# Wide loads, rows read eight tiles ahead, and results fetched a step sooner in a cross-attention and mixture-of-experts kernel

## The chip, the cores and the metric

The kernel runs on one core of a Trainium2 chip. The metric is the device time of one execution in microseconds. Three runs of the kernel before gave 608.56 us as median (607.83 to 609.25).

The core has a tensor engine (PE, which does the matrix products), a vector engine (DVE), a scalar engine (ACT), a general engine (POOL, GpSimd) and a sync engine (SP) that here only issues transfers. Transfers between device memory and on-chip memory run on 16 DMA engines. SP and ACT issue to hardware queues, which the profile numbers q1 and q10; POOL's transfers appear as q0.

## The reference

All tensors are float32. There are 4 batches of 512 tokens with 512 features, and a context of 1024 rows per batch.

```python
def layer(x, ctx):                      # x (4, 512, 512), ctx (4, 1024, 512)
    n = layernorm(x)
    q = fmap(n @ Wq.T)                  # fmap(a) = a + 1 if a > 0 else exp(a); 16 heads of 32
    gate = sigmoid(n @ Wg.T + bg)
    k, v = split(ctx @ Wkv.T)
    k = fmap(k)
    kv = einsum('bhsd,bhse->bhde', k, v)
    z = 1 / (einsum('bhld,bhd->bhl', q, k.sum(s)) + 1e-6)
    x = x + (einsum('bhld,bhde->bhle', q, kv) * z * gate) @ Wo.T
    n = layernorm(x)
    w, sel = top_k(n @ Wr, 2)           # 8 experts
    w = softmax(w)
    return x + sum(w[i] * (n @ We[sel[i]] + be[sel[i]]) for i in (0, 1))
```

## The kernel before

Work is tiled by 128 rows. The program first does the attention of the four batches in order. For each batch, `kv_tiles` (L374) goes over eight context tiles: it loads a tile two steps ahead (`load_ctx`, three buffers), makes keys and values from it with 8 matmuls each for keys and for values (`half_tile`, L310), and adds their product to a running sum. Then come queries and gates from the transposed, normalized x (`query`, `gate`), the attention products (`products`), the output projection (`attention_out`, L477), and the routing (`choose`, L526, and `dispatch`, L580). `dispatch` writes each token's normalized row twice into the array `stream` in device memory, once in the region of each of its two experts, by indirect writes that POOL issues.

The experts then work on tiles of 128 rows of `stream` (`run`, L738). The first 17 tiles (EARLY) belong to the first three batches and run inside and after the last batch's attention. The 18 late tiles that are always there (SURE) follow once the last batch has been dispatched and the list of their rows has been computed on DVE (`listed`, L680). For each tile, SP reads the row number from that list, then issues four loads of 64 KB and one of 1 KB (`rows`, L742). DVE transposes the tile in 32x32 blocks (`turned`, L776), PE does four chunks of matmuls with the expert's weights (`expert`, L796), DVE adds the bias, and POOL scatters the 128 result rows to the array `result` (L818).

The results are collected while the late tiles run: at steps of a hand-written plan (`begins`, L932) the two results of 128 tokens are fetched (`fetch`, L871), added with their gates (`add`, L896) and stored (`store`, L911). A list `READ` (L46) says how many tiles must be done before a fetch. The last two fetches wait for all results.

All of SP's transfers stay in the program's order. `tc.keep_in_program_order` and `tc.issue_after` fix further orders by hand; the rest of each engine's order is found when the program is built. The buffers of expert rows are the context tiles' three and two of the values'.

Three layouts matter here. `load_rows` (L132) fills a weight in four loads of 32 partitions each, with 4 x 512 numbers in each partition; the expert weights use the same layout in a loop of their own (L382). The tiles of the experts are loaded in the same manner, four loads of 32 partitions with 4 x 128 numbers each (L756). `spread_moments` (L277) writes the means and the reciprocal deviations of x to device memory in two transfers of single numbers and reads them back in four, so that every partition has those of its rows.

Of the kernel before, what the change touches and what calls it, by code (L numbers as in the profile page):

```python
# [9 lines left out]
F32 = mybir.dt.float32  # L10
I32 = mybir.dt.int32
U32 = mybir.dt.uint32
AF = mybir.ActivationFunctionType
ALU = mybir.AluOpType
# [3 lines left out]
P = 128  # L18
B, L, S, D = 4, 512, 1024, 512
E, F = 8, 512  # L20
HD = 32
NC = D // P
NT = L // P
# [30 lines left out]
def xattn_moe_kernel(  # L54
# [32 lines left out]
    result = dram.tile([NOWHERE + 2 * L, F], F32, name="result")  # L87


    moments = dram.tile([B, HD, NT, P // HD, 2], F32, name="moments")  # L90


    def matmul(**operands):
# [8 lines left out]
    def load(dst, src):  # L102
        latest["load"] = nc.sync.dma_start(out=dst, in_=src)  # L103
        tc.keep_in_program_order(latest["load"])
# [27 lines left out]
    def load_rows(dst, w):  # L132


        for i in range(NC):
            load(dst[ts(i, HD)], w.rearrange("(c f) i n -> i f c n", f=HD)[i])

    wkv_sb = wpool.tile([P, NC, 2 * D], F32, tag="wkv", name="wkv_sb")
    wq_sb = wpool.tile([P, NC, D], F32, tag="wq", name="wq_sb")
# [3 lines left out]
    nc.gpsimd.memset(wr_sb, 0.0)  # L143
    bg_sb = wpool.tile([P, NC], F32, name="bg_sb")
    we_sb = wpool.tile([P, E, NC, F], F32, name="we_sb")
    we_rows = we.rearrange("e (c f) i n -> e i f c n", f=HD)

    ctx_tiles = {}

# [104 lines left out]
    def layernorm_stats(tiles):  # L254
        mv = small.tile([P, NT, 2], F32, tag="mv", name="mv")
        for t in range(NT):
            st = small.tile([P, 6], F32, tag="st", name="st")
            nc.vector.bn_stats(st, tiles[t])
            nc.vector.bn_aggr(mv[:, t, :], st)
        rstd = small.tile([P, NT], F32, tag="rstd", name="rstd")  # L260
        nc.scalar.activation(rstd, mv[:, :, 1], AF.Sqrt, bias=eps_sb)
        nc.vector.reciprocal(rstd, rstd)
        return mv, rstd

    def normalize(dst, xt, t, mv, rstd):
        nc.vector.tensor_scalar(
            dst, xt, mv[:, t, 0:1], rstd[:, t : t + 1], ALU.subtract, ALU.mult
        )

    def transposed(dst, src):  # L270

# [4 lines left out]

    def spread_moments(b, tiles):  # L277

        mv, rstd = layernorm_stats(tiles)
        for k, of in enumerate((mv[:, :, 0], rstd)):  # L280
            nc.gpsimd.dma_start(
                out=moments[b, :, :, :, k].rearrange("t n j -> j t n"), in_=of
            )
        ln = small.tile([P, NT, P // HD, 2], F32, tag="ln", name="ln", bufs=1)
        for i in range(NC):
            nc.gpsimd.dma_start(
                out=ln[ts(i, HD)].rearrange("t n j k -> t (n j k)"),
                in_=moments[b].rearrange("t n j k -> t (n j k)"),
            )
        return ln  # L290

    def normalized_T(xT, t, blocks, ln):

        rows = blocks[:, ts(t, D)].rearrange("p (j f) -> p j f", f=P)
        with tc.issue_after(latest["map"].ins):
            for j in range(P // HD):
                nc.vector.tensor_scalar(
                    rows[:, j], rows[:, j], ln[:, t, j, 0:1], ln[:, t, j, 1:2],
                    ALU.subtract, ALU.mult,
                )  # L300
            nc.vector.transpose(
                xT[:, :, ts(t, P)].rearrange("p c (j t) -> p j c t", t=HD),
                rows.rearrange("p j (c f) -> p j c f", f=HD),
            )
# [69 lines left out]
    def kv_tiles(b, lo, hi, between=None, inside=None):  # L374
        for s in range(lo, hi):
            nxt = (b, s + 2) if s + 2 < NS else (b + 1, s + 2 - NS)
            if nxt[0] < B and nxt not in loaded_ctx:
                loaded_ctx.add(nxt)
                ctx_tiles[nxt] = load_ctx(*nxt)
            if b in (1, 2) and s % 2 == 0:  # L380
                e = (b - 1) * E // 2 + s // 2
                for i in range(NC):  # L382
                    load(we_sb[ts(i, HD), e], we_rows[e, i])
            for e in (s,) if b else (2 * (s - NS // 2), 2 * (s - NS // 2) + 1):
                if e >= 0:
                    set_empty(b, e)
            if s == 0:
                sums[b] = pkv.tile([P, NC, 2 * P], F32, tag="kvs", name="kvs")
            k = made.pop(s) if s in made else keys(b, s)
            if (b, s) == (0, 0):  # L390
                made[1] = keys(0, 1)
            if inside is not None and s == lo:
                inside()
            v = values(b, s)
            if s > 0:
                kv_add(sums[b], s - 1, *pending[b])
            pending[b] = k, v
            if between is not None:
                between(s - lo)
        if hi == NS:  # L400
            kv_add(sums[b], NS - 1, *pending[b])
# [121 lines left out]

    routed = {}

    def choose(b, mv, rstd):  # L526

        rows = []
        batch = work.tile([P, NT, ROW], F32, tag="row", name="rows", bufs=1)
        for t in range(NT):  # L530
            row = batch[:, t, :]
            normalize(row[:, 0:D], xs[b][t], t, mv, rstd)
            nc.gpsimd.tensor_copy(row[:, D : D + 1], home[:, b * NT + t : b * NT + t + 1])
            rows.append(row)

# [202 lines left out]
    def run(lists, lo, n, early):  # L738
        why = "clamped to the tiles of the streams and to the experts where it is computed"
        no_i, row_i, ranked = lists  # L740

        def rows(j):  # L742


            row = nc.values_load(
                row_i[0:1, j : j + 1], [ET.SP], min_val=0, max_val=SLOTS,
                skip_runtime_bounds_check_because=why,
            )
            if (j if early else j + EARLY) % 5 < 3:
                xg = cpool.tile([P, ROW], F32, tag="cT", name="xg")  # L750
            else:
                xg = kvpool.tile([P, ROW], F32, tag="v", name="xg", bufs=2)
            of = small.tile([P, 2], F32, tag="of", name="of", bufs=8)
            rows_of = stream[ds(row, P), :]
            parts = []
            for i in range(NC):  # L756
                parts.append(
                    (
                        xg[ts(i, HD), 0:D].rearrange("t (j f) -> t j f", j=NC),
                        rows_of[:, ts(i, P)].rearrange("(j t) f -> t j f", t=HD),  # L760
                    )
                )
            parts.append((of, rows_of[:, D:ROW]))
            for dst, src in parts:
                load = nc.sync.dma_start(out=dst, in_=src)  # L765
                latest["load"] = load
                if early:
                    behind(load, written["stream"][: 2 * NT * (B - 1)], "tokens of the tile")
                    early_loads.append(load)
                    for put in scatters.get(B - 1, []):  # L770
                        tc.declare_no_dep(load.ins, put.ins, reason=full_already)
                else:
                    behind(load, written["stream"], "tokens of the tile")
            return xg, of
# [55 lines left out]


        loaded, ready = [], []
        if early:
            turned_rows = big.tile([P, 4, NC, P], F32, tag="xT", name="turned_rows")

        def after(what):
            return tc.issue_after(latest[what].ins) if what in latest else nullcontext()

        for j in range(lo - 5, n):
            if j + 5 < n:  # L840
                with after("load"):
                    loaded.append(rows(j + 5))
            if j >= lo:
                with after("turn"):
                    expert(j, *ready.pop(0))
            if j + 3 >= lo and loaded:
                with after("y"):
                    ready.append(turned(j + 3, *loaded.pop(0)))
            yield
# [76 lines left out]
    def plan(step, *what):  # L926
        at_step.setdefault(min(step, SURE), []).append(what)

    def queue_of(step):
        return nc.gpsimd if step < SURE - 5 else nc.scalar  # L930

    begins = (-3, -2, -1, 0, 5, 6, 7, 8, 10, 11, 14, 15, SURE - 2, SURE - 2)  # L932
    for g, (lo, hi, most) in enumerate(READ):
        for t in range(lo, hi):
            plan(begins[t], fetch, t, most, queue_of(begins[t]), g)
    for t, begin in enumerate(begins):
        step = begin + (3 if begin < SURE - 4 else SURE)
        plan(step, add, t, gates if step < SURE else gates_end)
        plan(step + 1, store, t, queue_of(step + 1))

    def also(j):
        for what, *of in at_step.pop(j, []):
# [3 lines left out]
    xT = new_xT()  # L946
    kv_tiles(0, 0, 3)
    for g, a, b, n in turned:
        load(bg_sb[b : b + n, g : g + 1], bg[a : a + n, g : g + 1])
        load(wo_sb[b : b + n, g, :], wo[a : a + n, g, :])  # L950
    ln = spread_moments(0, xs[0])

# [2 lines left out]
            normalized_T(xT, t, blocks, ln)  # L955

    kv_tiles(0, 3, NS, between)
    kv_blocks(sums[0])
    for b in range(B):
        more = b + 1 < B  # L960
# [60 lines left out]
            for _ in range(3):  # L1021
                next(early)
        attention_out(b, aT)
        choice = choose(b, *layernorm_stats(xs[b]))
        if more:

            def between(i):
# [47 lines left out]
    nc.vector.tensor_copy(soon_i, worst)  # L1075

    late = run(late_list, 0, SURE, False)
    for j in range(-5, SURE):
        if j < 0:
            next(early)  # L1080
        next(late)
        with tc.issue_after(latest["y"].ins):
            also(j)
# [77 lines left out]
```

## Time and profile before

| | |
|---|---|
| median of the runs | 608.56 us |
| the profiled execution's own time | 610.59 us |
| its span in the profile | 608.9 us |
| mean granted clock of PE | 0.984 |
| PE busy | 576.7 us, 95% |
| DVE, ACT, POOL busy | 289.6, 109.3, 120.5 us |
| moved by DMA | 109.87 MB, mean 180 GB/s |
| SP's queue q1, share of 16 engines | 49.0% |
| first matmul starts, last one ends | 4.45 us, 589.2 us |
| four narrow loads of each expert weight, eight experts | 32 loads of 256 KB |
| loads of expert rows | 140 of 64 KB |

How it is read: the page gives each engine's busy time, then the span in forty slices of 15.2 us with the busy tenths of each. The DMA row is the mean busy share of the 16 engines. A view of the chain follows the work that ended last back to what released it. A timeline gives the instructions of one engine with the idle time before them in brackets and what ended it. The DMA view of a window gives for each queue the packets, the MB, and the time that its packets took as a share of 16 engines.

### The profile page before, as it was taken

Reading aid. Unit: us, or ns where it says so; the run is one execution under the profiler, and the core shown is the slowest. Engines: PE = TensorE matmul, PEld = TensorE weight load, DVE = VectorE, ACT = ScalarE, POOL = GpSimd, SP = SyncE. Lnnn points to the kernel's source line nnn. Section 1 sums busy time; section 2 is a strip of 40 time slices with the busy share of each in tenths; the row PEclk is TensorE's granted clock in tenths of the full one; section 3 lists DMA queues with packets and bytes.
Section 4 is the critical chain, followed back from the end, with each engine's and each line's share of the span. In section 5 each row is a group of like instructions: output and inputs, shape, how many; then the busy total and the mean of one; then the engine's idle time right before and its main releaser. Section 6 shows DMA issues by size and latency. Waiting matters only on the chain.

```text
span 608.9 us, 6440 instructions
## 1 busy us (share of the span) xinstructions
PE 576.7 (95%) x1780; PEld 270.0 (44%) x1780; DVE 289.6 (48%) x732; ACT 109.3 (18%) x168; POOL 120.5 (20%) x289
## 2 busy tenths in 40 slices
PE   7989999999999999999999999999999999998950
PEld 3545544454555435445543454554344443443420
DVE  2215254354317443541564355128765579473863
ACT  1311241220313321122242121221300110000000
POOL 4230021000001510000061100003211237444630
PEclk9989999999999999999999999999999999999995
DMA  8979995374490698627338660952255444889866
GB/s 283 166 122 355 340 197 48 116 238 131 121 277 19 140 240 261 190 87 209 103 140 147 236 203 5 315 221 108 89 119 121 121 122 167 251 235 295 243 225 212
DMA packets 78933, 109.87 MB, mean 180 GB/s; under 512 B 13229, under 2 KB 39853, under 8 KB 78768
## 3 DMA queue, kind: packets, MB, share of 16 engines
q1 hardware_dynamic: 68112, 79.91, 49.0%
q0 software_dynamic: 8336, 24.29, 12.2%
q10 hardware_dynamic: 2448, 5.24, 2.6%
q8 instruction: 15, 0.25, 0.2%
q14 instruction: 22, 0.18, 0.1%
HBM read 50.19 MB, written 59.96 MB: 181 GB/s over the span
## 4 chain that ended last, share of the span: by engine, by line
PE 74%; DMA 9%; DVE 6%; SPq 4%; issue 4%; POOL 1%; DVEq 0%; ACTq 0%; POOLq 0%
PE pk L94 18%; PE pv L94 16%; PE pq L94 9%; PE po L94 9%; PE pg L94 7%; PE pe L94 5%; PE kvs L94 4%; DMA xg<-stream 4%; DMA cT<-in_cT_dram 3%; SPq L765 2%; SPq L103 1%; PE pn L94 1%; PE pt L97 1%; DMA result<-y,to 1%; DMA of<-stream 1%
## 5 line engine op out<-in xcount | busy, mean ns | idle before, releaser
L94 PE MATMUL pk<-wkv_sb,cT 128*128 128x512 f32 x256 | 119.4, 611 | 6.4 <-DMA cT<-in_cT_dram 6.4
L94 PE MATMUL pv<-wkv_sb,cT 128*128 128x512 f32 x256 | 115.2, 593 | 0.0
L250 DVE TENSOR_SCALAR ex<-pk 128x512 f32<-128x512 f32 x32 | 22.1, 692 | 135.1 <-PE pk L94 135.1
L94 PEld LDWEIGHTS pv<-wkv_sb,cT 128*128 128x128 f32 x256 | 48.4, 190 | 62.3 <-issue 59.8
L94 PEld LDWEIGHTS pk<-wkv_sb,cT 128*128 128x128 f32 x256 | 48.0, 196 | 60.9 <-issue 53.4
L94 PE MATMUL pe<-we_sb,xgT 128*128 x144 | 62.8, 594 | 3.9 <-DVE xgT L782 3.9
L94 PE MATMUL pe<-we_sb,turned_rows 128*128 x136 | 60.4, 596 | 1.9 <-DVE turned_rows L782 1.5
L94 PE MATMUL pg<-xT,wg_sb 128*128 128x512 f32 x128 | 56.7, 595 | 0.0
L94 PE MATMUL pq<-xT,wq_sb 128*128 128x512 f32 x128 | 56.6, 596 | 0.0
L94 PE MATMUL po<-wo_sb,aT 128*128 128x512 f32 x128 | 55.6, 592 | 0.0
L818 POOL DMA_INDIRECT result<-y,to x35 | 36.4, 1041 | 94.0 <-DVE y L814 91.3
L251 ACT ACTIVATE ex<-ex 128x512 f32<-128x512 f32 x48 | 30.2, 629 | 137.5 <-DVE ex L250 117.3
L330 POOL MEMSET v<- 128x4 f32 x32 | 3.3, 108 | 245.4 <-PE kvs L94 245.3
L94 PEld LDWEIGHTS pe<-we_sb,xgT 128*128 128x128 f32 x144 | 27.1, 190 | 39.4 <-issue 32.2
L624 POOL DMA_INDIRECT stream<-rows,slot x32 | 32.9, 1027 | 51.7 <-DVE acc L587 22.2
L94 PEld LDWEIGHTS kvs<-v,k 128*128 128x128 f32 x256 | 33.3, 191 | 16.0 <-issue 14.2
L94 PEld LDWEIGHTS pe<-we_sb,turned_rows 128*128 128x128 f32 x136 | 25.2, 190 | 34.0 <-issue 29.9
L94 PEld LDWEIGHTS pg<-xT,wg_sb 128*128 128x128 f32 x128 | 24.0, 190 | 32.1 <-issue 32.1
L94 PEld LDWEIGHTS po<-wo_sb,aT 128*128 128x128 f32 x128 | 24.1, 190 | 29.2 <-issue 28.7
L94 PEld LDWEIGHTS pq<-xT,wq_sb 128*128 128x128 f32 x128 | 23.8, 190 | 27.3 <-issue 27.3
L94 PE MATMUL kvs<-v,k 128*128 128x129 f32 x256 | 34.1, 275 | 0.0
L252 DVE SCALAR_TENSOR_TENSOR k<-pk,ex 128x512 f32<-128x512 f32 x32 | 22.1, 691 | 21.6 <-ACT ex L251 21.6
(183 smaller groups left out, 459.7 us busy)
## 6 DMA issues: line engine op xcount, KB each, us to landing
stream<-empty SPq DMA_DIRECT2D x24, 1028.0 KB
stream<-empty SPq DMA_DIRECT2D x8, 1285.0 KB
xg<-stream SPq DMA_DIRECT2D x140, 64.0 KB
we_sb<-in_we_dram SPq DMA_DIRECT2D x32, 256.0 KB
cT<-in_cT_dram SPq DMA_DIRECT2D x31, 256.0 KB
y<-result POOLq DMA_DIRECT2D x10, 512.0 KB
x<-in_x_dram SPq DMA_DIRECT2D x16, 256.0 KB
blocks<-in_x_dram SPq DMA_DIRECT2D x16, 256.0 KB
```

Of the source, the lines that this page charges most:

```text
L94: tc.keep_in_program_order(nc.tensor.matmul(**operands))
L97: tc.keep_in_program_order(nc.tensor.transpose(dst, src, ident))
L103: latest["load"] = nc.sync.dma_start(out=dst, in_=src)
L250: nc.vector.tensor_scalar(ex, src, 0.0, None, ALU.min)
L251: nc.scalar.activation(ex, ex, AF.Exp)
L252: latest["map"] = nc.vector.scalar_tensor_tensor(dst, src, 0.0, ex, ALU.max, ALU.add)
L330: nc.gpsimd.memset(v[:, :, P : P + 1], 1.0)
L624: put = nc.gpsimd.indirect_dma_start(out=stream, out_offset=bass.IndirectOffsetOnAxis(ap=slots[i][:, t, :], axis=0), in_=rows[t], in_offse ...
L765: load = nc.sync.dma_start(out=dst, in_=src)
L818: put = nc.gpsimd.indirect_dma_start(out=result, out_offset=bass.IndirectOffsetOnAxis(ap=home_i, axis=0), in_=y, in_offset=None, bounds_ch ...
```

## The change

- `load_rows` loads chunk by chunk: four loads of 128 partitions with 512 numbers each, in place of four of 32 partitions. The expert weights go through it as well. A tile of expert rows is loaded in four loads of 32 of its rows each, spread over 128 partitions.
- The late tiles are loaded eight tiles ahead in place of five. Four further buffers come from the row buffer of the last batch's `choose` (`more`).
- The reciprocal deviations are put beside the means, and one transfer writes both to device memory, in runs of eight numbers.
- The loads of `bg` leave SP's queue for POOL's.
- The fetches of token tiles 4 to 9 move one step ahead, those of 10 and 11 two steps; the stores of tiles 8 and 9 go to SP's queue, and tiles 10 and 11 are added and stored within the steps.

```diff
@@ wide loads of weights
-        for i in range(NC):
-            load(dst[ts(i, HD)], w.rearrange("(c f) i n -> i f c n", f=HD)[i])
+        for c in range(NC):
+            load(dst[:, c, :], w[ts(c, HD)].rearrange("f i n -> i f n"))
...
-                for i in range(NC):
-                    load(we_sb[ts(i, HD), e], we_rows[e, i])
+                load_rows(we_sb[:, e], we[e])
@@ statistics
-    moments = dram.tile([B, HD, NT, P // HD, 2], F32, name="moments")
+    moments = dram.tile([B, HD, P // HD, NT, 2], F32, name="moments")
...
-        rstd = small.tile([P, NT], F32, tag="rstd", name="rstd")
-        nc.scalar.activation(rstd, mv[:, :, 1], AF.Sqrt, bias=eps_sb)
-        nc.vector.reciprocal(rstd, rstd)
-        return mv, rstd
+        dev = small.tile([P, NT], F32, tag="rstd", name="dev")
+        nc.scalar.activation(dev, mv[:, :, 1], AF.Sqrt, bias=eps_sb)
+        nc.vector.reciprocal(mv[:, :, 1], dev)
+        return mv
...
-        for k, of in enumerate((mv[:, :, 0], rstd)):
-            nc.gpsimd.dma_start(
-                out=moments[b, :, :, :, k].rearrange("t n j -> j t n"), in_=of
-            )
+        nc.gpsimd.dma_start(out=moments[b].rearrange("t j n k -> j t (n k)"), in_=mv)
@@ late tiles
+        many_ahead = not early and lo == 0
...
-            if (j if early else j + EARLY) % 5 < 3:
+            if many_ahead and (j - lo) % 9 < 4:
+                xg = more[:, (j - lo) % 9, :]
+            elif (j - lo) % 9 < 7 if many_ahead else (j if early else j + EARLY) % 5 < 3:
                 xg = cpool.tile([P, ROW], F32, tag="cT", name="xg")
...
-            for i in range(NC):
+            for j in range(P // HD):
                 parts.append(
                     (
-                        xg[ts(i, HD), 0:D].rearrange("t (j f) -> t j f", j=NC),
-                        rows_of[:, ts(i, P)].rearrange("(j t) f -> t j f", t=HD),
+                        xg[:, ts(j, P)],
+                        rows_of[ts(j, HD), 0:D].rearrange("t (i f) -> i t f", i=NC),
                     )
                 )
...
+        ahead = 8 if many_ahead else 5
+        if many_ahead:
+            more = work.tile([P, NT, ROW], F32, tag="row", name="more", bufs=1)
...
-        for j in range(lo - 5, n):
-            if j + 5 < n:
+        for j in range(lo - ahead, n):
+            if j + ahead < n:
                 with after("load"):
-                    loaded.append(rows(j + 5))
+                    loaded.append(rows(j + ahead))
...
     late = run(late_list, 0, SURE, False)
+    for _ in range(3):
+        next(late)
@@ results
-    def queue_of(step):
-        return nc.gpsimd if step < SURE - 5 else nc.scalar
+    def queue_of(step, behind=nc.scalar):
+        return nc.gpsimd if step < SURE - 6 else behind
 
-    begins = (-3, -2, -1, 0, 5, 6, 7, 8, 10, 11, 14, 15, SURE - 2, SURE - 2)
+    begins = (-3, -2, -1, 0, 4, 5, 6, 7, 9, 10, 12, 13, SURE - 2, SURE - 2)
...
-        plan(step + 1, store, t, queue_of(step + 1))
+        plan(step + 1, store, t, queue_of(step + 1, nc.sync if step < SURE - 4 else nc.scalar))
@@ bias of the gate
-        load(bg_sb[b : b + n, g : g + 1], bg[a : a + n, g : g + 1])
         load(wo_sb[b : b + n, g, :], wo[a : a + n, g, :])
...
     kv_tiles(0, 3, NS, between)
+    for g, a, b, n in turned:
+        nc.gpsimd.dma_start(out=bg_sb[b : b + n, g : g + 1], in_=bg[a : a + n, g : g + 1])
```

## The prediction

> **What bounds the kernel now.** I read the page first, for the engine shares and the forty slices.
>
> ```profile
> span 608.9 us, 6440 instructions
> ...
> PE 576.7 (95%) x1780; PEld 270.0 (44%) x1780; DVE 289.6 (48%) x732; ACT 109.3 (18%) x168; POOL 120.5 (20%) x289
> ...
> PE   7989999999999999999999999999999999998950
> ...
> DMA  8979995374490698627338660952255444889866
> ```
>
> TensorE is busy in all but 32 us. What an edit can save lies in the gaps: 4.45 us before the first matmul, a gap near 38 us, small ones after 515 us, and the 19.7 us after the last matmul. DMA is nearly full at the start (first six slices) and in the late tiles (slices 34 to 37). Between, it has room.
>
> Then the chain of waits, in order of time, around the gap near 38 us:
>
> ```profile
> 26.61 12.30 DMA cT<-in_cT_dram
> 38.91 0.14 issue
> 39.05 5.37 PE pk L94 x8
> 44.42 3.43 PE pv L94 x8
> ```
>
> The fifth context tile, issued at 26.61, lands at 38.9; TensorE had run dry at 37.05. It loses 2.0 us waiting and then 1.9 us, because the first eight matmuls after the gap take 5.37 us instead of 3.43. The load is slow because wg, wq and the x blocks stand before it on SP's queue.
>
> Next, TensorE's timeline at the end. A tile of the experts is 8 matmuls, 3.43 us.
>
> ```profile
> 515.56 7.13 PE L94 MATMUL pe<-we_sb,turned_rows 128*128 x16 [1.48 <-DVE turned_rows L782]
> 522.53 7.03 PE L94 MATMUL pe<-we_sb,xgT 128*128 x16
> 530.13 31.17 PE L94 MATMUL pe<-we_sb,xgT 128*128 x72 [0.58 <-DVE xgT L782]
> 562.91 20.87 PE L94 MATMUL pe<-we_sb,xgT 128*128 x48 [1.60 <-DVE xgT L782]
> 585.47 3.70 PE L94 MATMUL pe<-we_sb,xgT 128*128 x8 [1.70 <-DVE xgT L782]
> ```
>
> Late rows arrive just in time: in 66 us the gaps are 1.48+0.58+1.60+1.70 = 5.4 us. That is all that loading further ahead can win.
>
> Last, the DMA queues in four windows (0 to 10, 5 to 15, 15 to 20, 515 to 575 us); columns: packets, MB, share of 16 engines.
>
> ```profile
> q10 hardware_dynamic: 576, 0.26, 10.2%
> ...
> q1 hardware_dynamic: 1809, 3.29, 100.6%
> ...
> q1 hardware_dynamic: 603, 1.10, 104.1%
> ...
> q0 software_dynamic: 3062, 10.43, 50.0%
> q1 hardware_dynamic: 11804, 4.35, 34.4%
> ...
> y<-result POOLq DMA_DIRECT2D x10, 512.0 KB
> xg<-stream SPq DMA_DIRECT2D x69, 64.0 KB
> out_dram<-y POOLq DMA_DIRECT2D x7, 256.0 KB
> result<-y,to POOLq DMA_INDIRECT x18
> ```
>
> A share times 16 times the window is engine time. 5 to 15 us, 128-partition loads: 161 us for 3.29 MB, 100 ns for each 2 KB row. 15 to 20 us, wg and wq into 32 partitions: 83 us for 1.10 MB, 155 ns a row. 512 B rows: 16.3 us for the 512 rows of q10, 32 ns; late, 330 us for some 8,500 rows of q1, 39 ns with the small packets counted in. I take 34 ns.
>
> **The wide loads.** `load_rows` and the tile loads keep their bytes and row sizes (2 KB, 512 B) and their counts (4 a weight, 4 a tile), but each now fills 128 partitions. Two rules pull apart. The Trainium skill, "SBUF — State Buffer", section "Door 1: The DMA port swizzle", says that 32 partitions reach 8 of 16 ports; the 155 ns beside 100 ns fit. By that alone a wide wg or wq load takes 8 rows x 100 ns = 0.8 us of each engine instead of 1.24 us: 3.5 us for the eight.
>
> The rule that speaks against the change is in "DMA: Bandwidth & Descriptors", section "Why a DMA increments its semaphore by 16 and not by 1": a DMA is spread over the largest number of engines, up to 16, that divides the slowest dimension of both sides, and on the hardware queues these are the lowest-numbered. Before, the source is 32 x 4 x 512: 16 engines. After, `"f i n -> i f n"` makes it 4 x 32 x 512, and `"t (i f) -> i t f"` makes a tile's 4 x 32 x 128. Slowest dimension: 4. So each load would run on four engines, always the same four. No load on SP's or ACT's queue before has so short an outer dimension, so no row here shows it. I take this rule: it is about the descriptor split itself, and the other one presumes 16 engines. It prices the parts so:
>
> *Start.* wg and wq: 8 loads x 32 rows x 84 to 100 ns (84 is the median of the 2 KB packets in the trace's packet records, without the crowding of 16 full engines) = 22 to 26 us on those four engines, instead of 8 x 8 x 155 ns = 9.9 us. The loads before them are done near 13.5 us (4.3 MB moved by 15 us, of which 3.75 MB are theirs). wg then ends at 24 to 26 us; the fourth context tile, needed at 29.1, just makes it; wq ends at 37 to 39; the blocks (128 rows of 512 B an engine, 4 to 5 us) and the fifth context tile end at 43 to 45 and land at 44.5 to 47. Before: 38.9. I take +6 us on the path, between +2 and +10.
>
> *Expert weights.* Four loads hold four engines for 4 x 32 x 100 ns = 12.8 us instead of 5. They come every second context step (15.5 us), with 1.6 us of context tiles and two zero fills (5.8 us at 2056 B a row, 32 rows an engine each). That is 20 us in 15.5 us for two such pairs, then the gate and query stretch drains it. A context tile is issued two steps before use, with at most 14 us ahead of it: slack about 5 us, so nothing. Without that slack each pair would cost about 5 us: up to +15.
>
> *Early tiles.* A tile needs 128 x 34 ns = 4.4 us of four engines; before, SP's issue set 3.0 us a tile. Tile 0 comes about 1.5 us later, and it is on the path (its transposition stands before the attention products on DVE). The next three are needed 4.3 us and then 3.4 us apart, and po's 13.7 us lets loads catch up. +1 us (0 to +5).
>
> *Late tiles.* Loads start at 515, when the row list is done, as before. 18 x 4.4 us = 78 us on four engines. On the same engines lies their share of results: 50.0% of 60 us = 30 us. Sum 108 us, so the last tile lands near 515 + 108 + 2 = 625 and is transposed then instead of at 584.7: +40 us. By 32 ns and 25 us of other traffic it is +26; by 39 ns and 36 us, +54. TensorE's 62 us of late matmuls lie under it.
>
> **The other parts.** *Eight ahead, nine buffers:* SP's requests can run further ahead, but the first waits for the row list as before, and the `more` buffer was read by the last batch's row scatters, which each late load waits for anyway. Nothing while four engines are the limit. *Issue order of SP:* still five DMAs a tile, about 2.9 us, below 4.4. *Statistics in one write:* one POOL issue fewer per batch (1.5 to 2.0 us), 32 B runs instead of 4 B. On POOL, wg's copies now stand before that write and so wait for wg (25 us instead of landing early); behind it wait the ones-column of v 2, needed near 36, and the four reads of the moments, needed by DVE after the blocks. Hidden by TensorE's context work; if not, a few us at 36. *Bias loads:* seven issues leave SP (4.3 us together, TensorE not waiting) and go to POOL between 8.5 and 18 us, where it was idle for 9.6 us; at POOL's 0.5 to 1.7 us each they take 4 to 12 us and end before wg lands. Nothing. *Results sooner:* tiles 4 to 9 are fetched one step, 10 and 11 two steps earlier. On POOL the fetch can wait for a scatter landing, with the next scatter behind it; five y buffers cover that. Tiles 10 and 11 leave the tail: 1.5 MB less there, at about 400 GB/s 3.8 us of DMA, of which I count -2 us (0 to -4); the chain scatter, fetch, add, store stays.
>
> **Sum.** +6 +1 +40 -2 = +45 us. The profiled execution has a span of 608.9 us (610.6 with what lies around it); the median of the runs is 608.56, so 608.6 + 45 = 653.6; I say 653.
>
> **Rivals.** *A: all 16 engines move the wide loads.* Then the start wins 2.0 + 1.9 us (the tile lands 3.5 us or more sooner), late gaps lose perhaps 3 of 5.4 us, the tail 1 to 2 us: 600, between 597 and 608. For it: the 155 ns rows, which are then gone. Against: the source's outer dimension. It decides from about 10 engines up: 512 rows x 34 ns / 10 = 1.7 us a late tile, with 30/18 = 1.7 us of results, is TensorE's 3.43 us. *B: four engines, but late results and loads hide each other* (requests eight ahead let the loads start during the last early tiles, or rows run well under 30 ns): +4 to +10, 613 to 618. Against: the row list is not ready before 513.6. *C: four engines, and the expert weights also starve TensorE of context tiles:* +15 more and crowded late rows: 695 and up. *D: TensorE or DVE becomes the bound through added work:* there is none, the DVE instructions are as many as before.
>
> **How the numbers follow.** Four engines as summed 0.70 (its own range 625 to 690), A 0.17, B 0.06, C 0.07. Range 614 to 695: it holds the likeliest case, B's upper part and C's lower edge, some 0.8; A stays out. A change under 0.2% can't be told from none here. Slower: 0.70 + 0.06 + 0.07 = 0.83; A's 0.17 is 0.14 faster and 0.03 within.
>
> **What would show it.** On the changed page, DMA share in late slices far below 0.8 while TensorE has idle slices; DVE's transposition of late rows waiting for its load some 2 to 3 us a tile; late loads of one tile landing 4 us or more apart; the first gap near 38 us grown to 6 us or more; the last matmul near 635. In A the share stays, 2 KB rows of wg and wq cost 100 ns over all engines, and the gap at 38 us is gone. I am wrong if the loads spread over 16 engines, whatever the source's order.

## The result and the profile after

The changed kernel takes 674.88 us (673.79 to 676.76), in the same session as 608.9 us for the kernel before: a ratio of 1.109 (95% interval 1.106 to 1.112). The forecast was 653, slower, in a range of 614 to 695. The profiled execution took 673.79 us with a span of 672.1, so 63.2 us of span are to be accounted for.

From the page of the changed kernel:

```profile
span 672.1 us, 6433 instructions
...
PE 599.0 (89%) x1780; PEld 277.4 (41%) x1780; DVE 291.9 (43%) x732; ACT 108.9 (16%) x168; POOL 114.1 (17%) x292
...
PE   7939999999979999997999999998899998768760
...
DMA  7478980363551656345065526631233446565655
```

TensorE has idle slices in four places (slice 3; slices 12 and 19; slices 28 and 29; the late tiles from slice 34 on), and none of them has a full DMA row. The mean share of 16 engines in the late slices is 0.5 to 0.6, where it was 0.8 to 0.9. A few full engines would look like that in a mean over 16; whether they were full is taken up below.

The chain of waits, in order of time (start, duration, what), at the first two places:

```profile
40.19 7.82 DMA cT<-in_cT_dram
48.15 6.71 PE pk L94 x8
54.86 3.43 PE pv L94 x8
...
184.13 11.36 DMA x<-in_x_dram
...
199.32 1.88 PE pl L94 x8
```

The fifth context tile comes at 48 us; its values start at 54.86 instead of 44.42: 10.4 us lost. At 184 us the next batch's x is issued. It lands 11.4 us later, its statistics start on DVE, and only then does the router's product `pl` run. `pl` does not need the next batch's x. It needs `share`, a copy that ACT makes of `ps`, and PE had finished `ps` at 193.3. ACT's timeline says what stood in between, the square root of the next batch's statistics (`dev`):

```profile
198.50 0.30 ACT L260 ACTIVATE dev<-mv,eps_sb 128x4 f32<-128x4 f32 x1 [5.06 <-DVE mv L258]
198.70 0.56 ACT L545 COPY share<-ps 128x512 f32<-128x512 f32 x1
```

In the kernel before, ACT made the copy first, and the square root came 12 us later, at 195.61:

```profile
183.03 0.59 ACT L552 COPY share<-ps 128x512 f32<-128x512 f32 x1 [1.25 <-PE ps L94]
```

And TensorE's timeline of the changed kernel, later places:

```profile
472.70 6.08 PE L94 MATMUL pe<-we_sb,turned_rows 128*128 x8 [3.99 <-DVE aT L465]
...
605.92 13.12 PE L94 MATMUL pe<-we_sb,xgT 128*128 x24 [6.22 <-DVE xgT L778]
...
647.08 5.40 PE L94 MATMUL pe<-we_sb,xgT 128*128 x8 [3.56 <-DVE xgT L778]
```

Comparing the start of the same work in both traces gives a ledger. Each row is the growth of the delay since the row before.

| place | same work starts, before and after | lost here | forecast |
|---|---|---|---|
| start, values of the fifth context tile | 44.42, 54.86 | 10.4 | +6 |
| end of batch 0 (queries after dispatch) | 192.38, 210.41 | 7.6 | 0 |
| end of batch 1 | 304.86, 332.03 | 9.1 | 0 |
| early tiles, to the output projection | 457.15, 490.29 | 6.0 | +1 |
| late tiles, last matmul ends | 589.2, 652.5 | 30.2 | +40 |
| tail | 19.7 long, 19.6 long | -0.1 | -2 |

The sum is 63.2 us, the difference of the spans. After each long pause the first matmuls also run slower: the eight after 472.70 take 6.08 us instead of 3.60, the sixteen of `pq` after the pause at 199 take 8.80 us instead of 7.11, and the granted clock of the span is 0.944 where it was 0.984. So the rows of the ledger hold more than the pauses alone.

### The profile page after: what moved, and what is told of

It reads as the page before. It is cut to its first block, busy times and chain, and to the rows that moved or that the text cites. A ratio compares the mean times of both kernels' runs of the same rounds, so it can differ in the third digit from the quotient of the medians.

```text
span 672.1 us, 6433 instructions
## 1 busy us (share of the span) xinstructions
PE 599.0 (89%) x1780; PEld 277.4 (41%) x1780; DVE 291.9 (43%) x732; ACT 108.9 (16%) x168; POOL 114.1 (17%) x292
## 4 chain that ended last, share of the span: by engine, by line
PE 64%; SPq 11%; DMA 11%; DVE 6%; issue 5%; POOL 1%; ACT 0%; DVEq 0%; another core or an unknown queue 0%; POOLq 0%; ACTq 0%
PE pk L94 15%; PE pv L94 14%; PE pq L94 8%; PE po L94 8%; SPq L761 7%; PE pg L94 6%; PE pe L94 5%; DMA xg<-stream 4%; SPq L103 3%; DMA x<-in_x_dram 3%; PE kvs L94 3%; DMA cT<-in_cT_dram 1%; PE pn L94 1%; DMA result<-y,to 1%; POOL result L814 1%
## 5 line engine op out<-in xcount | busy, mean ns | idle before, releaser
L94 PE MATMUL pk<-wkv_sb,cT 128*128 128x512 f32 x256 | 121.1, 619 | 15.1 <-DMA cT<-in_cT_dram 10.6
L94 PE MATMUL pe<-we_sb,xgT 128*128 x144 | 74.0, 670 | 22.6 <-DVE xgT L778 22.5
L94 PE MATMUL pe<-we_sb,turned_rows 128*128 x136 | 62.8, 616 | 5.5 <-DVE aT L465 4.0
L94 PE MATMUL pq<-xT,wq_sb 128*128 128x512 f32 x128 | 61.2, 635 | 0.0
L94 PEld LDWEIGHTS pe<-we_sb,xgT 128*128 128x128 f32 x144 | 29.5, 213 | 67.1 <-DVE xgT L778 33.7
L250 ACT ACTIVATE ex<-ex 128x512 f32<-128x512 f32 x48 | 30.2, 629 | 159.4 <-DVE ex L249 136.2
L94 PEld LDWEIGHTS pq<-xT,wq_sb 128*128 128x128 f32 x128 | 25.6, 205 | 30.2 <-issue 29.9
L94 PEld LDWEIGHTS po<-wo_sb,aT 128*128 128x128 f32 x128 | 24.1, 190 | 29.2 <-issue 28.7
```

Source lines behind the costliest of these rows:

```text
L94: tc.keep_in_program_order(nc.tensor.matmul(**operands))
L250: nc.scalar.activation(ex, ex, AF.Exp)
```

## Experiments

### Which part costs, and is it the engines or the width?

Four kernels on one chip, beside 607.93 us for the kernel before. The first undoes both kinds of wide load and leaves the rest of the change.

```diff
+        for i in range(NC):      # e1: load_rows, as before
+            load(dst[ts(i, HD)], w.rearrange("(c f) i n -> i f c n", f=HD)[i])
+                        xg[ts(i, HD), 0:D].rearrange("t (j f) -> t j f", j=NC),   # e1, e2, e4: tiles
+                        rows_of[:, ts(i, P)].rearrange("(j t) f -> t j f", t=HD),
```

> The changed kernel with all wide loads made narrow again (32 partitions, source outer dimension 32); rows eight ahead, one write of the statistics, bias loads on POOL and earlier results stay. Theory (four DMA engines per wide load): all of the +66 us goes, and what the other parts win remains: about 603 us (597 to 608). Rival 1 (the wide writes themselves are slow, whatever the engines): the same. Rival 2 (the loss is in the other parts: POOL's queue order, nine buffers, fetches ahead): stays near 660 to 675 us.

Measured: 604.82 us, ratio 0.995 (0.993 to 0.997). The whole loss lies in the wide loads. What is left is slightly faster than the kernel before (0.5%).

> Only the weights (wg, wq, eight expert weights) are wide, tiles narrow, the rest as changed. From the trace of the changed kernel the start lost 10.4 us and the two batch boundaries 7.6 and 9.1 us: the theory expects the run of e1 plus 27 us, about 630 us (622 to 638), with the two waits of 5 us before the router's product pl in place and no late gaps. Rival 2: as e1. If the losses of the weights were only a consequence of something in the tiles, about 605.

Measured: 633.56 us, 28.7 over e1.

> Only the tiles of expert rows are wide, weights narrow, the rest as changed. The trace of the changed kernel lost 6.0 us in the early tiles and 30.2 us in the late ones: theory expects e1 plus 36 to 40 us, about 640 us (632 to 648), late tiles about 5.3 us apart instead of 3.43. The sum of the two parts (e2 - e1) + (e3 - e1) should be near the whole loss of 66 to 72 us, as both lie on the same path one after the other.

Measured: 639.90 us, 35.1 over e1. The two parts together make 63.8 us, a little under the 66 to 72 that were expected. The whole change is 70.1 over e1 by the medians of two sessions, so some 6 us come only with both.

The fourth keeps the weights wide. Only their order in device memory differs, so that the source of a load is 128 rows, one after the other:

```diff
-            load(dst[:, c, :], w[ts(c, HD)].rearrange("f i n -> i f n"))   # source 4 x 32 x 512
+            load(dst[:, c, :], w[c])                                       # source 128 x 512
...
+        v = w.reshape(*w.shape[:-3], NC, HD, NC, w.shape[-1])              # by_block, as the arrays are laid
+        return v.swapaxes(-3, -2).reshape(*w.shape[:-3], NC, P, w.shape[-1])
```

> Weights wide, with the same bytes to the same places, but laid out in device memory so that the source is 128 rows of 512 (outer dimension 128): by the theory 16 engines move it. Tiles narrow, the rest as changed. Theory: the start's gap before the fifth context tile shrinks or goes, so 0 to 5 us below e1: about 600 us (595 to 606). Rival 1 (writing 128 partitions at once is slow by itself): like e2, about 630 us.

Measured: 606.23 us, ratio 0.997 (0.995 to 0.999). Same bytes, same 128 partitions, same four loads a weight, and 27 us less than e2. Rival 1, that writing 128 partitions is slow by itself, is out for the weights. It is also not below e1, as was expected; why comes with the statistics, below.

The number of engines can be read from the page's count of packets on SP's queue (packets, MB, share). First e1:

```profile
q1 hardware_dynamic: 67776, 80.43, 46.8%
```

e2, with 40 wide loads of weights:

```profile
q1 hardware_dynamic: 67296, 80.43, 41.8%
```

e3, with 140 wide loads of tiles:

```profile
q1 hardware_dynamic: 66096, 80.42, 43.7%
```

e4, with 40 wide loads whose source is 128 rows:

```profile
q1 hardware_dynamic: 67776, 80.43, 44.6%
```

The bytes are equal, the rows are equal, and yet e2 has 480 packets fewer, 12 for each of 40 loads, and e3 has 1680 fewer, 12 for each of 140. e4 has none fewer. In the packet records it is packets of 4 bytes that are missing. If a load sends one such packet for each engine it uses, the wide loads from a 4 x 32 source used 16 - 12 = 4 engines.

The share of the engines confirms it. From 14 to 16 us SP's queue moves wg. First e1 (narrow), then e2 (wide, source 4 x 32), then e4 (wide, source 128 rows):

```profile
q1 hardware_dynamic: 219, 0.40, 105.8%
...
q1 hardware_dynamic: 95, 0.19, 26.2%
...
q1 hardware_dynamic: 396, 0.72, 102.1%
```

e2 keeps 26% of 16 engines busy, which is four, and moves half of what the narrow loads move. e4 keeps all 16 busy and moves 0.72 MB instead of 0.40. So the wide layout does give what the ports promised, 93 ns of an engine for a 2 KB row instead of 173, but only from a source that lets 16 engines share it; and even then the kernel gains nothing, because nothing on the path waited for it. Which four engines they are, no record here shows.

### The two batch boundaries

The forecast had the expert weights at nothing. e5 makes them alone wide; e6 is e5 with another queue for x.

```diff
+                for c in range(NC):                                        # e5, e6; wg, wq and tiles narrow
+                    load(we_sb[:, e, c, :], we[e, ts(c, HD)].rearrange("f i n -> i f n"))
...
-            load(xt, x[b, t])
+            if b > 0:                                                      # e6 alone
+                tc.keep_in_program_order(nc.scalar.dma_start(out=xt, in_=x[b, t]))
```

> Only the eight expert weights are wide; wg, wq and the tiles narrow, the rest as changed. Theory: the start is as in e1, the two batch boundaries lose 7.6 and 9.1 us as in the changed kernel: e1 plus 16 us, about 621 us (616 to 626), with a wait of 5 us before pl at both. If the loss at the boundaries was a late consequence of the slow start, about 605.

Measured: 620.94 us (before: 607.58), 16.1 over e1. TensorE's timeline of e5 has both waits again, this one and one of 4.96 us at 306.38:

```profile
184.88 1.88 PE L94 MATMUL pl<-by_expert,share 128*128 128x8 f32 x8 [5.16 <-ACT share L546]
```

> As e5, but the x tiles of batches 1 to 3 are issued by ACT on its own queue instead of by SP behind the expert weights. Theory (the next batch's x stands behind the wide expert weights in the rings of four engines, its statistics hold DVE and ACT, and ACT's copy of share holds PE): both waits of 5 us go, about 606 us (604 to 610). Rival (the expert weights slow something else, the context tiles or DMA as a whole): stays near 621.

Measured: 607.19 us, ratio to before 0.999 (0.997 to 1.002). The waits before `pl` are gone, though the expert weights are loaded with the same wide loads; one wait of 2.0 us before `pv` at 219 is new. But e6 changes more than the queue. ACT issues x at 98 us instead of 169, and the order of ACT's work, which is found when the program is built, is again that of the kernel before: `share` at 179, the square root at 223. So e6 alone can't tell x's landing from that order.

e4 can. Its order is that of e5 (square root, then `share`), but its wide expert weights run on 16 engines. Its x, issued at 170.24, lets the statistics start at 177.07; that of e5, issued at 169.43, at 181.07. And `pl` hardly waits:

```profile
180.91 1.06 PE L94 MATMUL pl<-by_expert,share 128*128 128x8 f32 x8 [0.39 <-ACT share L545]
```

So two things meet. Four wide loads of an expert weight and a zero fill stand in SP's queue, and the next batch's x is issued behind them and lands 11 us later. And the built order sets its statistics on ACT in front of the copy of `share`: ACT stands at the statistics, and TensorE waits for `share`. No run has a late x with the old order; there the statistics would have had 12 us more. The order is the old one in every kernel here with narrow weights and the new one in all with wide expert weights except e6; why it is built so was not looked into. The difference between e2 and e5, 12.6 us, is the price of wg and wq at the start.

### The tiles: throughput or lateness?

e3 does not say why the tiles lose. If four engines simply can't move enough, there is a threshold below which wide tiles are free. e7 makes every second tile wide, e11 every fourth.

```diff
+            wide = j % 2 == 1            # e11: j % 4 == 1
-            for j in range(P // HD):
+            for j in range(P // HD if wide else 0):
...
+            if not wide:                 # the narrow loads of before
```

> Weights narrow; of the expert tiles those with an odd number are wide, those with an even number narrow; the rest as changed. A row of 512 B took 29 ns in the late slices of the changed kernel, so a wide tile holds four engines for 3.7 us, a narrow one 0.9, the results 1.7 us a tile: 8.0 us for two tiles beside TensorE's 6.86. Theory (throughput of the four engines): late tiles lose 18 x 0.57 = 10 us, about 616 us (610 to 620). Rival (a wide tile is late by itself, whatever else the four engines do): half of e3's 35 us, about 622.

Measured: 624.33 us, 19.5 over e1 (15.9 to 21.1 by the interval), nearer to the rival's 622 than to the theory's 616.

> As e7, but only every fourth tile of expert rows is wide. Results took 2.0 us a tile of each engine in e7 (47.0% of 60 us for 14 tiles), not the 1.7 of the expectation for e7. Theory (throughput of the four engines alone): (3.7 + 3 x 0.93) / 4 + 2.0 = 3.6 us a tile beside TensorE's 3.43 to 3.53, so 1 to 4 us over e1, about 607. Rival (a wide tile is late by itself, each costs its share): a quarter of 35 us, about 613.

Measured: 617.94 us (four runs, 613.86 to 620.33), 13.1 over e1 (9.0 to 16.6 by the interval). Throughput alone, as summed, is refuted: it gave 1 to 4. An equal share for each wide tile fits loosely: nine and five of the 18 late tiles are wide, which would make 17.6 and 9.8 us of e3's 35, both inside the intervals. TensorE's timeline of e11 shows where the waits are:

```profile
523.67 14.37 PE L94 MATMUL pe<-we_sb,xgT 128*128 x32 [1.70 <-DVE xgT L787]
540.59 15.70 PE L94 MATMUL pe<-we_sb,xgT 128*128 x32 [2.55 <-DVE xgT L787]
559.09 14.00 PE L94 MATMUL pe<-we_sb,xgT 128*128 x32 [2.80 <-DVE xgT L787]
574.63 14.03 PE L94 MATMUL pe<-we_sb,xgT 128*128 x32 [1.54 <-DVE xgT L787]
593.21 6.62 PE L94 MATMUL pe<-we_sb,xgT 128*128 x8 [4.55 <-DVE xgT L787]
```

Five waits, one before each of the five wide tiles (late tiles 1, 5, 9, 13, 17), with three narrow tiles without a wait after each. SP's and DVE's timelines of e11 have tile 5's loads and its transposition:

```profile
529.45 3.46 SPq L770 DMA_DIRECT2D xg<-stream  x4
...
539.82 0.71 DVE L787 STREAM_TRANSPOSE xgT<-xg 128x512 f32<-128x512 f32 x1 [4.54 <-DMA xg<-stream]
```

From the first issue to the transposition, which waits for the landing, it takes 10.4 us; 9.1 to 12.6 us for the five wide tiles. A late tile of e1, all narrow, lands 3.8 to 8.5 us after its first issue, about 6 us in the median. Why is this not covered when rows are asked for eight tiles ahead? SP's timeline of e1, tiles 5 and 17:

```profile
527.15 2.79 SPq L761 DMA_DIRECT2D xg<-stream  x4
...
570.77 1.98 SPq L761 DMA_DIRECT2D xg<-stream  x4
```

Twelve tiles in 43.6 us are 3.6 us a tile. TensorE takes 3.43. SP starts at 510.9, when the row list is ready; tile 0's matmuls start at 518.75, tile 5's at 536.3, tile 17's at 578.75. So SP is about 8 us in front at the start, 9 us at tile 5 and 8 us at tile 17, whatever the number of buffers. A narrow tile fits into that, a wide one comes 1.5 to 4.6 us late.

What holds SP is seen in the instruction records: its transfers signal on eight semaphores in turn, and each waits until the transfer that was issued eight before it has landed. (In e1 that held for each of the 239 pairs whose landing the trace has.) A tile is five transfers, so fewer than two tiles are ever under way. In e11 this makes a wide tile late for its successors too. The four issues of tile 11, which is narrow, take 5.95 us, because the second and the third stand until the last two loads of wide tile 9 have landed:

```profile
554.35 5.95 SPq L770 DMA_DIRECT2D more<-stream  x4
```

So SP gets further in front while TensorE waits, but loses that again: at tiles 4, 12 and 16 it is 8, 8 and 7 us ahead, and the wide tile after each is late like the first.

With all tiles wide, SP has a second limit. In the changed kernel its late tiles start 5.2 us apart in the mean (548.04 to 635.96 for 17 of them) and 4.2 us apart at the quickest, both more than TensorE's 3.43. The issue instruction itself takes longer. The expert weights show that it goes with the four engines and not with the width (SP's instructions, ns min/median/max, first and last start in us); first e2, then e4, which is as e1 (median 430):

```profile
L103 SPq DMA_DIRECT2D we_sb<-in_we_dram x32: 531/573/2517, 87.3 to 297.5; - x32
...
L103 SPq DMA_DIRECT2D we_sb<-in_we_dram x32: 427/430/1578, 73.5 to 275.7; - x32
```

For the loads of rows the medians are 317 ns in e1 and 548 in e3. At the same time the four engines are near full: 18 tiles x 128 rows x 29 ns are 67 us, and POOL's and ACT's queues take 40% of the engines in that stretch, 39 us of each if they are spread evenly; together 106 us of packet time in the 98 us from the first late issue to the last transposition (the times of packets overlap). Whether SP's pace or the full engines set the 5.2 us, no run here separates. That the eight transfers under way explain e7 and e11 in full is argued from e11's timelines, not tested by a run of its own.

### The other parts

> The kernel before with one part of the change alone: the statistics written in one transfer of eight-number runs. In e1 the wait for the fifth context tile near 38 us is gone. Theory: it went because the single-number writes no longer hold the engines while the x blocks load; then 2.0 + 1.9 us go here too, about 604.7 us (603 to 606). Rival: it went because the seven bias loads left SP's queue; then no change, 608.

e8 is the kernel before with the one write of the statistics alone, as in the change's diff. Measured: 603.59 us, ratio 0.992 (0.989 to 0.995), the lowest median of all kernels here, though its interval meets e1's. The gap near 38 us is gone, with the bias loads still on SP's queue, so the theory holds. The DMA view from 18 to 31 us, row GB/s in 40 parts of the window. Before:

```profile
GB/s 189 208 214 239 252 315 170 221 233 227 227 202 202 221 265 208 202 211 187 178 190 190 175 134 87 47 42 72 81 103 61 41 54 54 30 32 55 115 118 210
```

e8:

```profile
GB/s 176 258 240 176 214 176 164 189 151 227 221 214 189 189 233 221 239 214 199 191 187 205 199 221 199 183 179 162 140 137 145 188 181 202 183 186 183 180 197 213
```

While the 1024 single numbers were written, the x blocks beside them fell to 30 to 100 GB/s for 4 us, with the engines counted as busy. With runs of eight numbers they keep 137 and more. This is also why e4 wins nothing at the start over e1: the gap that faster loads would have closed was closed already, and e1's timeline has no wait there.

```diff
-        many_ahead = not early and lo == 0        # e9, e12: five ahead, the old buffers
+        many_ahead = False
-    begins = (-3, -2, -1, 0, 4, 5, 6, 7, 9, 10, 12, 13, SURE - 2, SURE - 2)
+    begins = (-3, -2, -1, 0, 5, 6, 7, 8, 10, 11, 14, 15, SURE - 2, SURE - 2)   # e10, with the old queues
```

> As e1 (all loads narrow, the other parts as changed), but the late rows five ahead in the old five buffers. In the trace of e1 the late gaps are 0.4 us, before 3.9 us after 520. If eight ahead is what closed them: e1 plus 2 to 4 us, about 607. If not (e8, with five ahead, shows gaps of 2.5 us and the same time as e1): within 1.5 us of e1, about 605.

Measured: 604.96 us, e1 within 0.2 us. Its profiled execution, the fastest of its twelve runs, has no late gap at all: the 144 late matmuls run through from 518.28 us. So it was not eight ahead that closed e1's gaps; what did stays open.

> As e1, but the results fetched and stored at the steps and on the queues of before. The prediction counted 2 us for the earlier fetches; in the trace of e1 the time from the last matmul to the end is 20.9 us, before 19.7. Prediction: e1 plus 2 us, about 607. Rival from the traces (what leaves the tail only shortens waits beside the chain of scatter, fetch, add, store): no change or 1 us less, 604 to 605.

Measured: 604.83 us, the same as e1 (604.82). The 2 us that were expected did not come: the results fetched sooner are worth nothing that can be measured.

> As e3 (tiles wide, weights narrow), but five ahead in the old five buffers. Theory (four engines set the pace and are fed either way): as e3, about 640 us (637 to 644). Rival (eight tiles of requests fill the rings and put late tiles behind others): below 632. If eight ahead gave cover against late tiles: above 646.

Measured: 638.78 us, as e3 (639.90). Eight ahead neither helps nor harms the wide tiles.

## Why the prediction was right, and where its sum was off

The direction and the cause held. The step that decided, four engines for a source whose slowest dimension is 4, is shown by the packet counts, by the 26% of 16 engines in e2, and by e4. The rule on the ports is not wrong either: e4's wide rows took 93 ns where e1's narrow ones took 173. But it presumes all engines, and what it promised wasn't on the path. The signs that were named came: DMA's share fell to 0.5 to 0.6 in late slices with idle TensorE, DVE's transpositions waited some 3 us a tile for their rows, and the first gap grew from 2.0 to 10.6 us.

That the number came within 22 us is partly luck. Four terms were 28 us too small together, and the late tiles' term was 10 us too large.

**Start, +6, measured 10.4.** Right mechanism, just outside the range of +2 to +10. The term for wg and wq is 12.6 us by itself (e2 less e5, both with the better write of the statistics); in the change that write gave part of it back.

**Expert weights, 0, measured 16.7.** This step failed. The prediction followed the context tiles behind the wide weights, found 5 us of slack, and stopped there. In that it was right: after the fifth tile of batch 0 no context tile made TensorE wait in the changed kernel. It did not ask what else SP issues behind the weights. The next batch's x lands late, and in the order in which the changed program is built its statistics stand in front of `share` on ACT. With x in time that order costs 0.4 us (e4), with x late 5 us and the slower matmuls behind it, twice (e5). Rival C had up to +15 for the expert weights, near the measured size, but by starved context tiles: another path.

**Early tiles, +1, measured 6.0.** Right place, too small. The prediction had tile 0 come 1.5 us later. In the changed kernel the first early tile makes TensorE wait 4.0 us where it waited 0.4, and the eight matmuls behind it take 2.5 us longer. In e3, without the wide weights, the wait is 2.6 us.

**Late tiles, +40, measured 30.2.** The four engines were as full as the sum had them. The row of 512 B was taken at 34 ns and takes 29 in the changed kernel; with 29 the prediction's own sum gives 67 + 30 + 2 = 99 us from the first late load to the last transposition, and it took 98. (The packet time of the results was nearer 39 than 30, so the fit to 1 us is no proof.) The limits of the range, +26 and +54, do not follow from their working: 32 ns with 25 us gives +31, 39 ns with 36 us gives +58. Two things are missing from the sum. SP's issue was taken at 2.9 us a tile, below the engines' 4.4; with wide loads it is 5.2 us in the mean and 4.2 at the quickest. And the sum knows no cost below full engines, where e7 and e11 show one for single wide tiles: a landing time of 9 to 13 us against a lead of 8.

**Eight ahead, 0.** Right, but not only for the reason given, which was the four engines: it holds with narrow loads as well (e9). With at most eight transfers of SP under way, fewer than two tiles are, whatever the number of buffers.

**Results sooner, -2, measured 0.** The tail of the changed kernel is as long as before, and e10 shows no gain. What left the tail was not on its chain of scatter, fetch, add and store.

**Statistics and bias loads.** The prediction gave the single write nothing. Alone it wins 4 us (e8), because its cost was paid by its neighbours in the queues. Moving the bias loads wins nothing that shows, as said: e8, which leaves them on SP's queue, is no slower than e1.

## What to carry to other kernels

Before a load is reshaped, look at the outermost dimension of both sides, not only at the partitions: here the same bytes into the same 128 partitions took 4 or 16 engines by the order of the source alone, and a mean DMA share of 0.5 hid it. When a transfer gets slower, follow every transfer behind it in the queue to the engine that waits for it, and compare its landing time with the lead that the issuing engine really has; buffers and a loop that says "eight ahead" do not make that lead when the issuing engine may have only eight transfers under way. A built order can change with an edit: here the next batch's statistics had moved in front of a copy that TensorE needs, and a late x held both. A transfer of many single numbers is paid for by those beside it.

## What the runs showed that was not expected

- A write of 1024 single numbers (4 KB in all) lowered the x blocks beside it from about 200 to 30 to 100 GB/s for some 4 us. Written in runs of eight numbers it did not, and the kernel won 4 us (e8).
- Nine buffers and a distance of eight tiles gave the same time as five and five, with narrow loads (604.82 and 604.96 us) and with wide ones (639.90 and 638.78 us).
- One wide tile in four cost 13 us, all wide cost 35: 2.6 us for each of five wide late tiles, less than 2 us for each of 18.
- A load that ran on four engines kept SP longer at its issue: 573 ns (median) for an expert weight instead of 430, 548 ns for rows instead of 317. The same wide load on 16 engines took 430.
- A change in the shape of the weights' loads changed the order in which ACT's work was built, with wide loads on 16 engines too (e4).
